# Row statistics finished by GpSimd, and the end of the last sequence's feed-forward part rearranged, in a recurrent fusion and ternary FFN kernel

## The chip, the cores and the metric

The kernel runs on one core of a Trainium2 chip. The metric is the device time of one execution in microseconds; less is better. Of the kernel before there are three timed runs, and one execution under the hardware profiler, from which all durations and instants below come. Instants are microseconds from the start of the profiled span. Engines are named as in the profile: PE (TensorE, matmuls; PEld are its weight loads), DVE (VectorE), ACT (ScalarE), POOL (GpSimd), SP (the engine that issues most DMAs).

## The reference

There are 8 sequences of 512 tokens with 512 features, in f32. In short (shapes left out):

```python
def recurrent(x):                     # both directions, 4 layers, the same weights
    h = x
    for i in range(4):
        z = sigmoid(h @ Wz[i].T + b[i]);  t = tanh(h @ Wh[i].T + b[i])   # Wz = Wh
        a = clip(1 - z, 1e-8, 1 - 1e-8)
        n = linear_scan(a, z * t)     # n[s] = a[s] * n[s-1] + z[s] * t[s]
        h = layernorm(n + (h if i > 0 else 0)) * gamma + beta
    return h
x = x + concat(recurrent(ln(x)), flip(recurrent(flip(ln(x))))) @ fusion_W.T + fusion_b
h = gelu(ln(x) @ ternary(W_fc).T)     # 512 -> 2048
x = x + (layernorm(h) * ln_w + ln_b) @ ternary(W_proj).T
```

`ternary(W)` makes -1, 0 and 1 out of the weights, by half the mean of their absolute values as the threshold. Each layer norm takes the mean and variance of a row (one token, all its features), adds 1e-5 to the variance and raises it to -0.5.

## The kernel before

**First part, to 1222 us: the recurrence and the fusion.** Features lie on the partitions, in four chunks of 128 (`c` or `o`), and the 512 tokens along the free axis, so that the scan of a chunk is one VectorE instruction. Sequences go in pairs; a pair has four streams (two sequences, two directions), and the layers go round the streams. One chunk of a layer is a *step*, in the code a `slot` (L439), about 4.3 us long: TensorE computes `u` (L461), ScalarE makes `a`, `t` and `z` of it (L478 to L480), VectorE clamps `a` (L484), multiplies `z` and `t` (L485), scans (L489) and adds the residual (L548).

The layer norm needs tokens on the partitions. For each of the four token tiles of a stream, TensorE transposes four blocks of `z` into a PSUM tile `pt` (L316, two buffers); VectorE takes `bn_stats` (L171) and `bn_aggr` (L173, `mv` holds mean and variance); then the eps is added (L177, `ve`, VectorE), GpSimd raises to -0.5 (L178, `rs`), VectorE negates the mean (L182, `nmu`), ScalarE multiplies the two (L188, `nmr`) and writes the normalised tile `tok` (L189), which frees `pt`. When four tiles are there, TensorE transposes them back (L325, `pf`), and ScalarE applies gamma and beta on the way to the state (L331). These pieces wait in two queues, `turns` and `backs`, with a due time in steps; `shares` (L258) gives each step one piece of a queue, or two where they are late or the step allows it. The order of all instructions is fixed by this code (a manual schedule); each engine runs its own in order. In a step the queued pieces come after the step's gate matmuls; VectorE does their statistics first and then the step's clamp, product and scan.

Three kinds of statistics go another way: those of x (`rx`, L391) and of the last layer (`rsv`, L354) end with the power and need no shift, and those of y come ahead of the feed-forward part and in it (`y_stats`, L923). The fusion reads `rsv` in L592. Weights are quantised in gaps.

**Second part, from 1222 us: the feed-forward part.** For each sequence `b` and each of 16 chunks `k` of the 2048 features, `fc` (L831) makes `ph` by eight matmuls (L836), then on ScalarE the gelu `g`, its square and the scaled `ghi`, and on VectorE two running sums `acc` (L851) and the rest `glo`. `proj` (L858) multiplies `ghi` and `glo` with the output weights, eight matmuls (L863) into the four token tiles `po`. The loop (L936) runs `fc` two chunks ahead of `proj` (`LAG`); in the last sequence two steps do two `fc` each, so that `token_stats` (L868), which transposes the sums and takes the statistics of the 2048 features, can come two steps before the end. The last two chunks' `proj` goes tile by tile: `center` (L893) has put the mean's part into the rows before, and `finish_last` (L915) adds each tile's scaled `po` and stores it by SP.

Of the kernel before, what the change touches and what calls it, by code (L numbers as in the profile page):

```python
# [9 lines left out]
F32 = mybir.dt.float32  # L10
F32R = mybir.dt.float32r
AF = mybir.ActivationFunctionType
ALU = mybir.AluOpType
# [3 lines left out]
P = 128  # L17
LN_EPS = 1e-5
# [6 lines left out]
def kernel(  # L25
# [26 lines left out]
    nc = tc.nc  # L52
    B, S, H = x.shape
    L = gru_wT.shape[0]
    F = fc_wT.shape[1]
    NC_ = H // P
    NT = S // P
# [6 lines left out]
    const = ctx.enter_context(tc.tile_pool(name="const", bufs=1))  # L64
    small = ctx.enter_context(tc.tile_pool(name="small", bufs=8))
# [11 lines left out]
    fusp = rec.enter_context(tc.tile_pool(name="fus", bufs=1))  # L77
# [29 lines left out]
    gb = const.tile([P, L, NC_], F32, name="gb")  # L107
    gam = const.tile([P, NC_], F32, name="gam")
    bet = const.tile([P, NC_], F32, name="bet")
    fb = const.tile([P, H], F32, name="fb")  # L110
    lnw = const.tile([P, NF], F32, name="lnw")
    lnb = const.tile([P, NF], F32, name="lnb")

# [2 lines left out]
    nc.vector.memset(warm, 0.0)  # L116
    ones = const.tile([P, P], F32, name="ones")
    nc.vector.memset(ones, 1.0)
    both = const.tile([P, NC_, 2, 64], F32, name="both")
    picks = []  # L120
    for i in range(2):
        s = const.tile([P, P], F32, name=f"fpick{i}")
        nc.vector.memset(s, 0.0)
        nc.vector.memset(s[64 * i : 64 * i + 1, :], 1.0 / H if i else 1.0)
        picks.append(s)
# [42 lines left out]
    def stats(src, name, rs=None, shift=True):  # L168

        st = small.tile([P, 6], F32, tag="st", name=f"st_{name}")  # L170
        nc.vector.bn_stats(st, src)  # L171
        mv = small.tile([P, 2], F32, tag="mv", name=f"mv_{name}")
        nc.vector.bn_aggr(mv, st)  # L173
        if rs is None:
            rs = small.tile([P, 1], F32, tag="rs", name=f"rs_{name}")
        ve = small.tile([P, 1], F32, tag="ve", name=f"ve_{name}")
        nc.vector.tensor_scalar(ve, mv[:, 1:2], LN_EPS, None, ALU.add)  # L177
        nc.gpsimd.tensor_tensor(rs, ve, mhalf, ALU.pow)  # L178
        if not shift:
            return rs, None  # L180
        nmu = small.tile([P, 1], F32, tag="nmu", name=f"nmu_{name}")
        nc.vector.tensor_scalar(nmu, mv[:, 0:1], -1.0, None, ALU.mult)  # L182
        return rs, nmu

    def normalise(dst, src, rs_nmu, name):
        rs, nmu = rs_nmu
        nmr = small.tile([P, 1], F32, tag="nmr", name=f"nmr_{name}")
        nc.scalar.activation(nmr, nmu, AF.Copy, scale=rs)  # L188
        nc.scalar.activation(dst, src, AF.Identity, bias=nmr, scale=rs)  # L189

    def ternary(dst, w, hi_lo):
# [11 lines left out]
    def load_y(b):  # L203

        for t in range(NT):
            xs["y", b, t] = xsp.tile([P, H], F32, tag="xs", name=f"xy_{b}_{t}")
            nc.sync.dma_start(out=xs["y", b, t], in_=x1[b][t])
# [3 lines left out]
    def y_chunk(b, toks, c, px):  # L211

        for t in range(NT):
            nc.tensor.transpose(px[:, ts(t, P)], toks[t][:, ts(c, P)], ident)  # L214

        def split():
            hi = zp.tile([P, S], F32R, tag="z", name=f"yhi_{b}_{c}")
            lo = zp.tile([P, S], F32R, tag="z", name=f"ylo_{b}_{c}")
            nc.scalar.copy(hi, px)
            nc.vector.tensor_tensor(lo, px, hi.bitcast(F32), ALU.subtract)  # L220
            ys.setdefault(b, []).append((hi, lo))
        return split
# [6 lines left out]
    with rec:  # L229
# [130 lines left out]
        rx, scale = {}, {}  # L360
# [430 lines left out]


    gpool = ctx.enter_context(tc.tile_pool(name="g", bufs=3, reuse_waits="tile"))
    partp = ctx.enter_context(tc.tile_pool(name="parts", bufs=5, reuse_waits="tile"))
    accp = ctx.enter_context(tc.tile_pool(name="acc", bufs=1, reuse_waits="tile"))
    ps_x = ctx.enter_context(tc.tile_pool(name="ps_x", bufs=2, space=PSUM, reuse_waits="tile"))
    ps_o = ctx.enter_context(tc.tile_pool(name="ps_o", bufs=1, space=PSUM, reuse_waits="tile"))
# [4 lines left out]
    for i in range(2):  # L802
        s = const.tile([P, P], F32, name=f"pick{i}")
# [25 lines left out]
    acc, po, first, stat = {}, {}, {}, {}  # L829

    def fc(b, k):  # L831
        ph = ps_f.tile([P, S], F32, tag="pf", name=f"ph_{b}_{k}")
        for c in range(NC_):
            w = fcq[k // NP_][:, c, ts(k % NP_, P)]
            for i in range(2):
                nc.tensor.matmul(  # L836
                    ph, lhsT=w, rhs=ys[b][c][i], start=(c == 0 and i == 0), stop=(c == NC_ - 1 and i == 1),
                )
        g = gpool.tile([P, S], F32, tag="g", name=f"g_{b}_{k}")
        nc.scalar.activation(g, ph, AF.Gelu)  # L840
        sq = gpool.tile([P, S], F32, tag="sq", name=f"sq_{b}_{k}")
        nc.scalar.activation(sq, g, AF.Square)
        ghi = partp.tile([P, S], F32R, tag="ghi", name=f"ghi_{b}_{k}")
        nc.scalar.activation(ghi, g, AF.Copy, scale=lnw[:, k : k + 1])
        if k == 0:
            first[b] = (g, sq)
        else:
            if k == 1:
                acc[b] = [accp.tile([P, S], F32, tag=f"acc{i}", name=f"acc{i}_{b}") for i in range(2)]
            for i, v in enumerate((g, sq)):  # L850
                nc.vector.tensor_tensor(acc[b][i], first[b][i] if k == 1 else acc[b][i], v, ALU.add)  # L851
        glo = partp.tile([P, S], F32R, tag="glo", name=f"glo_{b}_{k}")
        nc.vector.scalar_tensor_tensor(
            glo, g, lnw[:, k : k + 1], ghi.bitcast(F32), ALU.mult, ALU.subtract
        )
        return ghi, glo
# [11 lines left out]
    def token_stats(b):  # L868

        su = small.tile([P, 2, NT], F32, tag="su", name=f"su_{b}")  # L870
        for i, v in enumerate(acc.pop(b)):
            pst = ps_x.tile([P, 512], F32, tag="px", name=f"pst_{b}_{i}")
            for t in range(NT):
                nc.tensor.transpose(pst[:, ts(t, P)], v[:, ts(t, P)], ident)
            nc.vector.tensor_reduce(su[:, i, :], pst.rearrange("p (t f) -> p t f", t=NT), AX.X, ALU.add)
        nc.vector.tensor_scalar(su, su, 1.0 / F, None, ALU.mult)
        var = small.tile([P, NT], F32, tag="var", name=f"var_{b}")
        nc.vector.tensor_tensor(var, su[:, 0, :], su[:, 0, :], ALU.mult)
        nc.vector.tensor_tensor(var, su[:, 1, :], var, ALU.subtract)
        nc.vector.tensor_scalar(var, var, 0.0, LN_EPS, ALU.max, ALU.add)  # L880
        rs = small.tile([P, NT], F32, tag="rsg", name=f"rsg_{b}")
        nc.gpsimd.tensor_tensor(rs, var, mhalf.broadcast_to([P, NT]), ALU.pow)

        def last():
            nmr = small.tile([P, NT], F32, tag="nmrg", name=f"nmrg_{b}")
            nc.vector.scalar_tensor_tensor(nmr, su[:, 0, :], -1.0, rs, ALU.mult, ALU.mult)
            stat[b] = (rs, nmr)
            if b == B - 1:
                for t in range(NT):
                    center(b, t, xs["y", b, t])  # L890
        return last
# [8 lines left out]
    def store(b, t):  # L900
        nc.sync.dma_start(out=out[b, ts(t, P), :], in_=xs["y", b, t])
# [12 lines left out]

    def finish_last(b, t):  # L915
        row = xs["y", b, t]
        nc.vector.scalar_tensor_tensor(row, po[b][t], stat[b][0][:, t : t + 1], row, ALU.mult, ALU.add)
        store(b, t)

    rests = []  # L920
    found, ytok = {}, {}
# [12 lines left out]
    ends = B * NF  # L934
    todo = [(b, k) for b in range(B) for k in range(NF)]
    for j in range(ends):  # L936
        b, k = divmod(j, NF)
        late = []
        for _ in range(2 if ends - 4 <= j < ends - 2 else 1):
            if todo:  # L940
                waiting.append((*todo[0], *fc(*todo[0])))
                todo.pop(0)
        if j == ends - 2:
            late.append(token_stats(b))
        if k == 0 and b > 0:
            late.append(token_stats(b - 1))
        if b == 0 and 5 <= k < 5 + NC_ + 3:
            row_piece(k - 5)
        if b + 1 < B and k >= NF - NC_:
            px = ps_x.tile([P, S], F32, tag="px", name=f"py_{b + 1}_{k}")  # L950
            late.append(y_chunk(b + 1, ytok[b + 1], k - (NF - NC_), px))
        if j >= LAG:
            done = waiting.pop(0)
            proj(*done)
        for f in late:
            f()
        if rests:
            rests.pop(0)()
        if j >= LAG and done[1] == NF - 1:
            finish(done[0])  # L960
        at = 12 if b == 0 else 8
        if at <= k < at + NT:
            xt = xs["y", b, k - at]
            nc.vector.tensor_tensor(xt, xt, rows[1], ALU.add)
        if b + 1 < B:
            if k == 2:
                load_y(b + 1)
            if k in (6, 7):
                y_stats(b + 1, (2 * k - 12, 2 * k - 11))
            if k in (8, 9):  # L970
                y_tokens(b + 1, (2 * k - 16, 2 * k - 15))
# [47 lines left out]
```

## Time and profile before

| | |
|---|---|
| median of three runs | 1719.33 us (1719.25 to 1719.43) |
| the profiled execution's own time | 1719.44 us |
| its span, first to last instruction | 1717.4 us |
| TensorE clock granted | 1.00 throughout |
| busy: PE / DVE / ACT / POOL | 99% / 84% / 62% / 12% |
| GpSimd's power of a 128x1 tile (L178) | 317 times, about 0.64 us |
| `ve` (L177), `nmu` (L182) on VectorE | 0.15 us, 0.14 us each |
| `nmr` (L188) on ScalarE | 224 times, 0.29 us |

[...]the profile models their ends, so a busy TensorE may still lose time between two matmuls; it shows as a start later than the usual spacing. A line of the timeline gives the start, the duration, the engine, the line of the code, the operation, the tile written and those read, and in brackets the idle time before it and what ended it. A line of the waits gives who waited for whom, the total in us, how often, and the longest.

### The profile page before, as it was taken

The page shows a single profiled execution, that of the slowest core. Times are in us where ns is not written, and L with a number is a line of the kernel's source. Part 1 is how long each engine was busy: PE and PEld are TensorE (multiplying, and loading weights), DVE is VectorE, ACT ScalarE, POOL GpSimd, SP SyncE. Part 2 cuts the span into 40 slices and gives each one's busy share as a digit, 9 for nine tenths or more (in the row PEclk, how much of TensorE's full clock was granted, in tenths as well). Part 3 has the DMA queues.
Part 4 walks back from the last instruction along what each step waited for, and adds up shares of the span by engine and source line. Part 5 has one row for each costly group of instructions (what it writes and reads, how often), then busy time and mean ns, then how long its engine had stood idle before and what let it go on. Part 6 is the DMA issues. An engine that isn't in the chain of part 4 may idle for free.

```text
span 1717.4 us, 19766 instructions
## 1 busy us (share of the span) xinstructions
PE 1705.8 (99%) x6442; PEld 1042.8 (61%) x6442; DVE 1449.8 (84%) x2859; ACT 1072.3 (62%) x1851; POOL 214.5 (12%) x334
## 2 busy tenths in 40 slices
PE   9999999999999999999999999999999999999998
PEld 4455554555555455555545555554688888888887
DVE  7989989889998998999899899996568768768876
ACT  5898883468886246888624688861266566566654
POOL 2111111111111111111111111110000000000000
PEclk9999999999999999999999999999999999999999
DMA  7002221160000115000012200202201101100100
GB/s 270 19 25 81 99 86 43 56 202 1 1 13 19 56 59 199 1 1 19 13 55 68 105 15 35 74 1 98 74 1 49 50 1 50 50 19 32 50 19 31
DMA packets 46455, 91.75 MB, mean 53 GB/s; under 512 B 5264, under 2 KB 5264, under 8 KB 45328
## 3 DMA queue, kind: packets, MB, share of 16 engines
q1 hardware_dynamic: 45632, 89.18, 15.3%
q10 hardware_dynamic: 720, 1.31, 0.2%
q8 instruction: 51, 0.84, 0.2%
q14 instruction: 52, 0.43, 0.1%
HBM read 65.30 MB, written 25.17 MB: 53 GB/s over the span
## 4 chain that ended last, share of the span: by engine, by line
PE 85%; DVE 9%; issue 4%; ACT 1%; DMA 1%; POOL 0%; DVEq 0%; POOLq 0%; ACTq 0%; SPq 0%
PE u L461 33%; PE pu L582 12%; PE ph L836 12%; PE po L863 12%; PE pt L316 6%; PE u L504 5%; PE pf L325 4%; DVE z L489 2%; DVE st L171 1%; DVE z L485 1%; PE py L214 1%; DVE zf L489 1%; DVE z L548 1%; DVE a L484 1%; DMA xT<-in_xt_dram 0%
## 5 line engine op out<-in xcount | busy, mean ns | idle before, releaser
L461 PE MATMUL u<-h,gw 128*128 128x512 f32 x768 | 345.5, 592 | 0.0
L461 PE MATMUL u<-xT,gw 128*128 128x512 f32 x768 | 345.4, 593 | 0.0
L489 DVE TENSOR_TENSOR_SCAN z<-a,z 128x512 f32<-128x512 f32 x224 | 274.1, 1224 | 7.6
L840 ACT ACTIVATE g<-ph 128x512 f32<-128x512 f32 x128 | 76.4, 597 | 240.6 <-PE ph L836 240.6
L461 PEld LDWEIGHTS u<-h,gw 128*128 128x128 f32 x768 | 138.7, 190 | 139.2 <-issue 138.9
L461 PEld LDWEIGHTS u<-xT,gw 128*128 128x128 f32 x768 | 138.7, 190 | 139.2 <-issue 138.2
L478 ACT ACTIVATE a<-u,ngb 128x512 f32<-128x512 f32 x192 | 131.6, 685 | 142.2 <-PE u L461 141.6
L171 DVE BATCH_NORM_STATS2 st<-pt 128x6 f32<-128x512 f32 x256 | 177.1, 692 | 40.5 <-PE pt L316 40.1
L178 POOL TENSOR_TENSOR rs<-ve,mhalf 128x1 f32<-128x1 f32 x192 | 123.2, 642 | 702.8 <-DVE nmu L182 669.9
L863 PE MATMUL po<-pwq,ghi 128*128 128x512 f32 x512 | 203.5, 398 | 0.0
L836 PE MATMUL ph<-yhi,fcq 128*128 128x512 f32 x512 | 199.7, 390 | 0.0
L863 PE MATMUL po<-pwq,glo 128*128 128x512 f32 x512 | 199.6, 390 | 0.0
L836 PE MATMUL ph<-ylo,fcq 128*128 128x512 f32 x512 | 199.4, 389 | 0.0
L485 DVE TENSOR_TENSOR z<-z,t 128x512 f32<-128x512 f32 x224 | 153.4, 685 | 9.1 <-ACT z L480 9.1
L189 ACT ACTIVATE tok<-pt,nmr,rs 128x512 f32<-128x512 f32 x192 | 149.2, 777 | 6.4
L851 DVE TENSOR_TENSOR acc<-acc,g 128x512 f32<-128x512 f32 x112 | 77.3, 690 | 87.9 <-ACT g L840 87.0
L480 ACT ACTIVATE z<-u,gb 128x512 f32<-128x512 f32 x192 | 132.2, 689 | 0.0
L479 ACT ACTIVATE t<-u,gb 128x512 f32<-128x512 f32 x192 | 130.7, 681 | 0.0
L316 PEld LDWEIGHTS pt<-ident,z 128*128 128x128 f32 x640 | 78.6, 141 | 79.7 <-issue 47.7
L504 PE MATMUL u<-xT,gw 128*128 128x512 f32 x256 | 114.8, 593 | 0.8 <-DVE gw L711 0.8
L582 PE MATMUL pu<-fw,xT 128*128 128x512 f32 x256 | 115.2, 593 | 0.0
L582 PE MATMUL pu<-fw,h 128*128 128x512 f32 x256 | 115.1, 592 | 0.0
(147 smaller groups left out, 2558.5 us busy)
## 6 DMA issues: line engine op xcount, KB each, us to landing
xn<-in_x_dram SPq DMA_DIRECT2D x32, 256.0 KB, 4.4
xf<-in_x_dram SPq DMA_DIRECT2D x32, 256.0 KB, 5.5
x<-xf SPq DMA_DIRECT2D x32, 256.0 KB, 2.0
xy<-x SPq DMA_DIRECT2D x32, 256.0 KB, 4.4
out_dram<-xy SPq DMA_DIRECT2D x32, 256.0 KB, 2.0
xT<-in_xt_dram SPq DMA_DIRECT2D x7, 1024.0 KB, 7.5
fca<-in_fc_wT_dram SPq DMA_DIRECT2D x16, 256.0 KB, 3.0
pwa<-in_proj_wT_dram SPq DMA_DIRECT2D x16, 256.0 KB, 2.6
```

The costliest lines, as they stand in the source:

```text
L171: nc.vector.bn_stats(st, src)
L189: nc.scalar.activation(dst, src, AF.Identity, bias=nmr, scale=rs)
L316: nc.tensor.transpose(pt[:, ts(c, P)], zs[c][:, ts(t, P)], ident)
L461: nc.tensor.matmul(u, lhsT=gw[l][:, c, ts(o, P)], rhs=h[:, c, :], start=(c == 0), stop=(c == NC_ - 1),)
L478: nc.scalar.activation(a, u, AF.Sigmoid, bias=ngb[:, l, o : o + 1], scale=-1.0)
L480: nc.scalar.activation(z, u, AF.Sigmoid, bias=gb[:, l, o : o + 1])
L485: nc.vector.tensor_tensor(z, z, t, ALU.mult)
L489: nc.vector.tensor_tensor_scan(dst[:, d], a[:, d], z[:, d], 0.0, ALU.mult, ALU.add)
L504: nc.tensor.matmul(u, lhsT=gw[0][:, c, ts(o, P)], rhs=xT[b][:, c, :], start=(c == 0), stop=(c == NC_ - 1),)
L582: nc.tensor.matmul(pu, lhsT=hs[d][:, c, ts(t, P)], rhs=fw[:, d * NC_ + c, :], start=(c == 0), stop=(c == NC_ - 1),)
L836: nc.tensor.matmul(ph, lhsT=w, rhs=ys[b][c][i], start=(c == 0 and i == 0), stop=(c == NC_ - 1 and i == 1),)
L863: nc.tensor.matmul(po[b][t], lhsT=part[:, ts(t, P)], rhs=pwq[k // NP_][:, k % NP_, :], start=(k == 0 and i == 0), stop=(k == NF - 1 and i ...
```

## The change

Four things change.

- The eps (`ve`) is added by GpSimd for all statistics, in front of its power. The product of mean, `rs` and -1 (`nmr`) is made by GpSimd behind the power, in one instruction; VectorE's `nmu` and ScalarE's `nmr` go. `normalise` keeps only the activation.
- In the last sequence three steps do two `fc` each, in place of two, and one step earlier: `fc` leads `proj` by five chunks at the most. `token_stats` comes three steps before the end. `ghi` and `glo` get a sixth buffer.
- The last token tile is finished in two halves of 256 columns; the second half's store is issued by ScalarE's queue.
- `fb`, `both` and the two `fpick` tiles move from the pool that lasts to the end to one that ends with the first part.

```diff
-    fb = const.tile([P, H], F32, name="fb")
+    fb = fusp.tile([P, H], F32, name="fb")
...
-    both = const.tile([P, NC_, 2, 64], F32, name="both")
+    both = fusp.tile([P, NC_, 2, 64], F32, name="both")
...
-        s = const.tile([P, P], F32, name=f"fpick{i}")
+        s = fusp.tile([P, P], F32, name=f"fpick{i}")
...
         ve = small.tile([P, 1], F32, tag="ve", name=f"ve_{name}")
-        nc.vector.tensor_scalar(ve, mv[:, 1:2], LN_EPS, None, ALU.add)
+        nc.gpsimd.tensor_scalar(ve, mv[:, 1:2], LN_EPS, None, ALU.add)
         nc.gpsimd.tensor_tensor(rs, ve, mhalf, ALU.pow)
         if not shift:
             return rs, None
-        nmu = small.tile([P, 1], F32, tag="nmu", name=f"nmu_{name}")
-        nc.vector.tensor_scalar(nmu, mv[:, 0:1], -1.0, None, ALU.mult)
-        return rs, nmu
-
-    def normalise(dst, src, rs_nmu, name):
-        rs, nmu = rs_nmu
         nmr = small.tile([P, 1], F32, tag="nmr", name=f"nmr_{name}")
-        nc.scalar.activation(nmr, nmu, AF.Copy, scale=rs)
+        nc.gpsimd.tensor_scalar(nmr, mv[:, 0:1], rs, -1.0, ALU.mult, ALU.mult)
+        return rs, nmr
+
+    def normalise(dst, src, rs_nmr, name):
+        rs, nmr = rs_nmr
         nc.scalar.activation(dst, src, AF.Identity, bias=nmr, scale=rs)
...
-    partp = ctx.enter_context(tc.tile_pool(name="parts", bufs=5, reuse_waits="tile"))
+    partp = ctx.enter_context(tc.tile_pool(name="parts", bufs=6, reuse_waits="tile"))
...
     def finish_last(b, t):
         row = xs["y", b, t]
-        nc.vector.scalar_tensor_tensor(row, po[b][t], stat[b][0][:, t : t + 1], row, ALU.mult, ALU.add)
-        store(b, t)
+
+        for h in range(2 if t == NT - 1 else 1):
+            cols = slice(h * H // 2, (h + 1) * H // 2) if t == NT - 1 else slice(0, H)
+            nc.vector.scalar_tensor_tensor(
+                row[:, cols], po[b][t][:, cols], stat[b][0][:, t : t + 1], row[:, cols], ALU.mult, ALU.add
+            )
+            (nc.scalar if h else nc.sync).dma_start(out=out[b, ts(t, P), cols], in_=row[:, cols])
...
-        for _ in range(2 if ends - 4 <= j < ends - 2 else 1):
+        for _ in range(2 if ends - 6 <= j < ends - 3 else 1):
             if todo:
                 waiting.append((*todo[0], *fc(*todo[0])))
                 todo.pop(0)
-        if j == ends - 2:
+        if j == ends - 3:
             late.append(token_stats(b))
```

## The prediction

> **What bounds the kernel now.** I read the page's busy times first, then the waits, then the timeline of one ordinary step, and then listed, from the timeline, every place where TensorE's matmuls start later than their normal spacing.
>
> ```profile
> PE 1705.8 (99%) x6442; PEld 1042.8 (61%) x6442; DVE 1449.8 (84%) x2859; ACT 1072.3 (62%) x1851; POOL 214.5 (12%) x334
> ```
>
> The waits (who waited for whom, us in total, times, longest):
>
> ```profile
> POOL rs L178 <- DVE nmu L182: 669.9, 181, 24.2
> ...
> ACT nmr L188 <- POOL rs L178: 64.9, 49, 7.2
> ...
> PEld pt L316 <- ACT tok L189: 26.7, 86, 0.9
> ```
>
> TensorE is busy 1705.8 of 1717.4 us, and its matmuls follow each other at fixed spacings (429 ns for a 128x512 one with `gw`, 109 ns for a transpose, 227 ns in the feed-forward part). Adding up what exceeds these spacings gives only 17 us: 5.6 before 60 us, 2.3 from there to 120 us, the rest scattered. So there is little to win. What can be lost is in the last line: TensorE waits 86 times for a row tile `tok` that ScalarE makes out of the row statistics. VectorE and GpSimd matter only through that.
>
> ```profile
> 439.81 0.60 PE L325 MATMUL pf<-ident,tok 128*128 128x128 f32 x4
> ...
> 440.75 0.18 DVE L173 BATCH_NORM_AGGREGATE mv<-st 128x2 f32<-128x6 f32 x1
> 441.04 0.15 DVE L177 TENSOR_SCALAR ve<-mv 128x1 f32<-128x1 f32 x1
> 441.11 0.14 DVE L182 TENSOR_SCALAR nmu<-mv 128x1 f32<-128x1 f32 x1
> 441.17 0.42 DVE L484 TENSOR_SCALAR a<-a 128x512 f32<-128x512 f32 x1
> ...
> 441.33 0.65 POOL L178 TENSOR_TENSOR rs<-ve,mhalf 128x1 f32<-128x1 f32 x1 [3.65 <-DVE nmu L182]
> 441.50 0.68 DVE L485 TENSOR_TENSOR z<-z,t 128x512 f32<-128x512 f32 x1
> 442.02 0.29 ACT L188 ACTIVATE nmr<-nmu,rs 128x1 f32<-128x1 f32 x1
> 442.22 1.22 DVE L489 TENSOR_TENSOR_SCAN z<-a,z 128x512 f32<-128x512 f32 x1
> 442.35 0.78 ACT L189 ACTIVATE tok<-pt,nmr,rs 128x512 f32<-128x512 f32 x1
> ```
>
> This is one step (4.31 us), and its neighbours are alike. From the end of `mv` (440.93) to the start of `tok` it takes 1.42 us. The `tok` of the step before ended at 438.82 and was the last of its four; its transpose, the fourth of those from 439.81 on, comes at 440.14, 1.32 us later. This margin is the number that decides.
>
> ```profile
> 38.14 1.21 DVE L489 TENSOR_TENSOR_SCAN z<-a,z 128x512 f32<-128x512 f32 x1
> 38.24 1.45 POOL L178 TENSOR_TENSOR rs<-ve,mhalf 128x1 f32<-128x1 f32 x1 [0.59 <-DVE nmu L182]
> ```
>
> Here the same GpSimd power takes 1.45 us, because it begins inside a scan and ends 0.34 us after it. I paired all 317 powers with the VectorE instruction under way at their start. Beside `bn_stats` (input in PSUM) 81 take 0.55 us. Beside the clamp L484 172 end 0.41 us after its end; so do those beside the products and sums of two SBUF tiles (16 of L851 and L485: 0.9 us).
>
> [...] VectorE shows no price for it: the product after the clamp takes 0.684 us with a power waiting and 0.685 without. [...] three powers in a row at 13.5 us start 0.52 and 0.63 us apart.
>
> **The change, part by part.** The order of instructions on TensorE is unchanged but for eight matmuls near the end; VectorE loses 541 small instructions, ScalarE 224, GpSimd gains 541.
>
> (1) *VectorE and ScalarE are relieved.* Start to start, `mv` to the clamp is 0.42 us now; without `ve` and `nmu` some 0.12: 0.3 us less per statistic. ScalarE loses an `nmr` of 0.29 us. That pays only where they hold TensorE up: around 40 us, and at 72 to 88 us, where two statistics fall in each step and VectorE is full.
>
> (2) *The chain runs through GpSimd three times.* No row shows a GpSimd `tensor_scalar` of 128x1. Bounds: 0.29 us (the affine select of 128x128 on GpSimd) and 0.55 (the power). I take 0.45, 0.31 when it had waited for the port, and 0.06 for the wait on its own result (between 0.03 and 0.14, the handovers seen). With the `mv` end as zero, in the step above: the clamp now runs from -0.08 to 0.34. `ve` starts at 0.13, gets the port at 0.34, is done at 0.65. The power asks at 0.85, while the product runs (0.53 to 1.22, held by ScalarE's `z`), and ends at 1.22+0.41=1.62. `nmr` then asks inside the scan (1.25 to 2.47) and ends at 2.78: `tok` starts at 2.8 in place of 1.42, **1.4 us later**. A shorter instruction hardly helps, since the ends of VectorE's instructions set the times. As `tok` then holds up ScalarE's next gates and so the next product, the power of the next step finds the port free: about 0.7 us. I let 1.4 and 0.7 alternate.
>
> With two statistics in a step (371 us) the first chain runs beside the second's `bn_stats`, but the second queues behind it: its `ve` waits for the scan, its power for the residual sum, and `tok` starts about 4.7 us after the first `mv`, in place of 2.6: **2.0 us later**.
>
> Now the margins. For 47 groups of back transposes (L325 and the first of y) I took the time from the end of the last `tok` to where TensorE would have been free. Five have 0.24 us or less (193, 228, 526, 824, 1126 us): 5.1 us more stall. Four have 0.5 to 0.75: 1.9. Three have 0.89: 0.9. Twenty have about 1.32: nothing or 0.1 each, 1.3. Sum 9.1. For the transposes into a PSUM buffer that `tok` frees, margins are 4.9 us in ordinary steps; they are short where two go in one step. That comes three times, at 321-379, 619-677 and 917-975 us, with margins of -0.2, 0, 0.55, -0.34 and 0.46 us: 0.7+1.5+0.5+1.3+0.2=4.2 each, 12.6 in all (the fourth cut from 2.0, since the stall before it gives time). At 72-110 us the VectorE-bound stall of 0.75 us in a step turns into one on GpSimd of 1.2, and four steps with 0.25 to 0.8 us to spare get one: +4. At 30-52 us 1.1 us is won at the 1.43 us stall on the scan, and lost again at the next `tok`; the first scale comes 0.3 later: 0. Sum 25.7. The margins are those of a trace in which nothing else stalls, and each stall lets the other engines catch up: I take three quarters, **+19.3 us**.
>
> The power for the last layer (`rsv`) is read by L592 at least 1.1 us later, once, else over 5.6: free. The statistics of y in the feed-forward part are used two steps of 3.6 us later: free.
>
> (3) *FC chunks lead by five, token statistics one step earlier.*
>
> ```profile
> 1708.91 2.74 DVE L896 SCALAR_TENSOR_TENSOR xy<-row,nmrg,xy 128x512 f32<-128x512 f32 x4
> ...
> 1711.57 2.72 DVE L917 SCALAR_TENSOR_TENSOR xy<-po,rsg,xy 128x512 f32<-128x512 f32 x4
> ...
> 1712.61 0.39 PE L863 MATMUL po<-pwq,glo 128*128 128x512 f32 x1
> ```
>
> The last matmul ends at 1713.0, VectorE at 1714.29: the four centerings hold it up. They come 1.8 us earlier (eight matmuls of 227 ns), so VectorE follows TensorE. The sixth buffer keeps the lead from waiting. (4) *Last tile in halves*: the second ends at about 1713.1+0.8=1713.9, 0.4 earlier; its store goes past SP on ScalarE's queue, which is idle then, and saves another 0.1 (bounds 0 and 0.3; the store of a whole tile lands in 2.0). Together **-0.5 us**. (5) `fb`, `both` and the picks move to a pool that ends with the first part: no instruction, no wait at the seam (0.4 us there now) that I can see: 0.
>
> Sum: +18.8. The profiled execution took 1719.44 us, 2.1 us outside its 1717.35 of span; the median is 1719.33. So 1719.3+18.8 = **1738**.
>
> **Rivals.** *A, faster, 1716:* GpSimd's small instructions slip between VectorE's, `tok` comes at most 0.2 us later, and the relief decides: -1.8 us at 72-88, -1.5 at the start, -0.9 in the three places, -0.5 at the end, +1 at the five tight groups: -3.7. It decides as long as `mv` to `tok` stays under about 1.7 us. Against it: the 172 powers that did wait for the clamp. *B, same, 1720:* the 1.3 us margin hides nearly all; five tight groups at 1 us cancel against the 4.5 of relief and end. *C, worse, 1761:* shifts of 1.7/1.0, pairs 2.6 us late, and no catching up: 16+19+7=42 us. For it: in a pair step GpSimd needs up to 4.8 us of a 4.75 us step. That part of the edit has no effect is excluded by the instruction order.
>
> **Numbers.** Forecast 0.60 (shift of 1.0/0.5 gives 1728, 1.7/1.0 gives 1751), C 0.16, B 0.13, A 0.11. About 0.2% (3.4 us) can be told from no change. The range leaves out A and the far part of C: 1719 to 1758. Faster 0.11, same 0.13, slower 0.76.
>
> **What would show it.** Right: from `mv` to `tok` 2 us and more; GpSimd's second and third instruction ending 0.3 to 0.4 us after a VectorE product or scan; the wait of `pt` and `pf` for `tok` several times 26.7 us, most of it at 320-379, 619-677, 917-975; VectorE's end 0.4 us nearer to the last matmul. Wrong: `mv` to `tok` near 1.6 us, or that wait unchanged. A stall at the seam near 1222 us would make the layout the cause.

## The result and the profile after

| | before | after |
|---|---|---|
| median | 1719.37 us (1719.25 to 1719.43, 4 runs) | 1739.7 us (1736.4 to 1741.07, 4 runs) |
| the profiled execution's own time | 1719.44 us | 1739.72 us |
| its span | 1717.35 us | 1737.93 us |
| ratio after/before | | 1.0116, 95% interval 1.0098 to 1.0133 |

The changed kernel is 20 us slower. The four runs of after lie further apart than those of before: the mean TensorE clock on record is 0.997 or 0.998 in three of them and 1.000 in the one of 1736.4 us. I come back to that at the end.

In after's code the lines behind the statistics have numbers two lower, up to `finish_last`: the transposes `pt` and the back transposes `pf` are now L314 and L323, `tok` is L187, the clamp, product and scan L482, L483 and L487, the residual L546. `nmr` is now L182, on POOL.

The busy times of after, from its page:

```profile
PE 1710.7 (98%) x6442; PEld 1044.0 (60%) x6442; DVE 1395.0 (80%) x2319; ACT 1009.8 (58%) x1627; POOL 475.3 (27%) x875
```

VectorE lost 55 us of work and ScalarE 62, and GpSimd gained 261. But 317 `ve` at 0.22 us and 224 `nmr` at 0.27, which is what they take with no VectorE instruction beside them (see the durations further down), are only some 130. The other half is not work, it is waiting that the profile counts as busy, because it lies inside the instructions: in the mean the 256 `ve` of the streams take 0.31 us and the 192 `nmr` ahead of `tok` 0.55. TensorE's busy time grew by 5 us only; the span grew by 20.6. So TensorE waits more. The waits of after (who waited for whom, us in total, times, longest):

```profile
POOL ve L177 <- DVE mv L173: 716.5, 210, 22.5
...
ACT tok L187 <- POOL nmr L182: 201.4, 176, 7.6
...
PEld pt L314 <- ACT tok L187: 23.5, 24, 2.2
...
PE pt L314 <- ACT tok L187: 12.8, 14, 2.0
...
PEld pf L323 <- ACT tok L187: 10.4, 10, 2.8
...
PE pf L323 <- ACT tok L187: 8.0, 8, 2.6
```

The matmuls' own waits before:

```profile
PE pt L316 <- ACT tok L189: 2.5, 7, 0.6
...
PE pf L325 <- ACT tok L189: 0.4, 1, 0.4
```

`tok` waits 201 us for the new `nmr`. The weight loads' wait of `pt` for `tok`, which the prediction shows as 26.7 us in 86 waits, is smaller than before, 23.5 us in 24. What grew are the waits on TensorE's own lines: `pt` from 2.5 to 12.8 us and `pf` from 0.4 to 8.0. Together they grew by 17.9 us, most of the 20.6. The weight loads' two lines grew by 5 us only (28.8 to 33.9). They don't tell what was lost: before, they held 28.8 us, while the late starts of all matmuls add up to 17.2 us and the matmuls' own two lines to 2.9.

The same ordinary step in the timeline of after (start, duration, engine, line, operation):

```profile
443.91 0.18 DVE L173 BATCH_NORM_AGGREGATE mv<-st 128x2 f32<-128x6 f32 x1
444.01 0.40 DVE L482 TENSOR_SCALAR a<-a 128x512 f32<-128x512 f32 x1
444.18 0.31 POOL L177 TENSOR_SCALAR ve<-mv 128x1 f32<-128x1 f32 x1 [2.83 <-DVE mv L173]
...
444.54 0.69 DVE L483 TENSOR_TENSOR z<-z,t 128x512 f32<-128x512 f32 x1
444.57 1.09 POOL L178 TENSOR_TENSOR rs<-ve,mhalf 128x1 f32<-128x1 f32 x1
...
445.27 1.22 DVE L487 TENSOR_TENSOR_SCAN z<-a,z 128x512 f32<-128x512 f32 x1
...
445.77 0.80 POOL L182 TENSOR_SCALAR nmr<-mv,rs 128x1 f32<-128x1 f32 x1
...
446.60 0.78 ACT L187 ACTIVATE tok<-pt,nmr,rs 128x512 f32<-128x512 f32 x1 [1.42 <-POOL nmr L182]
...
448.21 0.18 DVE L173 BATCH_NORM_AGGREGATE mv<-st 128x2 f32<-128x6 f32 x1
...
448.87 0.57 POOL L178 TENSOR_TENSOR rs<-ve,mhalf 128x1 f32<-128x1 f32 x1
...
449.14 0.69 DVE L483 TENSOR_TENSOR z<-z,t 128x512 f32<-128x512 f32 x1 [0.44 <-ACT z L478]
...
449.54 0.43 POOL L182 TENSOR_SCALAR nmr<-mv,rs 128x1 f32<-128x1 f32 x1
...
449.87 1.22 DVE L487 TENSOR_TENSOR_SCAN z<-a,z 128x512 f32<-128x512 f32 x1
450.00 0.78 ACT L187 ACTIVATE tok<-pt,nmr,rs 128x512 f32<-128x512 f32 x1 [0.22 <-POOL nmr L182]
```

Each GpSimd instruction begins while a VectorE instruction runs, and ends just after that one's end: `ve` at 444.49 after the clamp (444.41), the power at 445.66 after the product (445.23), `nmr` at 446.57 after the scan (446.49). From the end of `mv` (444.09) to `tok` it is 2.51 us, against 1.42 before. In the next step (448.39 to 450.00) it is 1.61. Over all 192 statistics of this kind the mean is 2.18 us, 1.51 before (the medians are 1.95 and 1.42).

In a step with two statistics (after's timeline; the first `mv` ended at 380.96, this is the chain of the second, whose `mv` ended at 381.83):

```profile
382.78 1.22 DVE L487 TENSOR_TENSOR_SCAN z<-a,z 128x512 f32<-128x512 f32 x1
382.96 1.06 POOL L177 TENSOR_SCALAR ve<-mv 128x1 f32<-128x1 f32 x1
...
384.04 0.69 DVE L546 TENSOR_TENSOR z<-z,xT 128x512 f32<-128x512 f32 x1
384.10 1.05 POOL L178 TENSOR_TENSOR rs<-ve,mhalf 128x1 f32<-128x1 f32 x1
...
385.26 0.27 POOL L182 TENSOR_SCALAR nmr<-mv,rs 128x1 f32<-128x1 f32 x1
...
385.56 0.78 ACT L187 ACTIVATE tok<-pt,nmr,rs 128x512 f32<-128x512 f32 x1 [1.87 <-POOL nmr L182]
...
386.39 0.66 PE L314 MATMUL pt<-ident,z 128*128 128x128 f32 x4 [1.99 <-ACT tok L187]
```

`ve` comes after the first chain's `nmr` (to 382.87) and waits out the scan, the power waits out the residual sum, and TensorE stands for 2 us at `pt`, since `tok` frees its buffer.

Adding up, as in the prediction, how much later than their usual spacing TensorE's matmuls start: 17.2 us before, 38.8 after, +21.6. The tail, from the start of the last matmul to the end of the span, shrank from 4.74 to 4.17 us. Together +21.0; the span says +20.6, and I can't place the 0.4 between them. By place (the rows from lists of the larger stalls, hence 21.2 in sum):

| where | before | after | difference |
|---|---|---|---|
| to 60 us | 5.6 | 6.0 | +0.4 |
| 72 to 110 us, stalls | 2.0 | 5.7 | +3.7 |
| back transposes (`pf` and the first of y), from 120 us | 0.8 | 7.7 | +6.9 |
| the three places with two statistics in a step | 2.1 | 9.5 | +7.4 |
| TensorE at half clock, twice | 0 | 3.4 | +3.4 |
| the tail | 4.74 | 4.17 | -0.6 |

And the end of the span, from after's timeline:

```profile
1733.77 0.39 PE L861 MATMUL po<-pwq,glo 128*128 128x512 f32 x1
1734.19 0.88 DVE L918 SCALAR_TENSOR_TENSOR xy<-po,rsg,xy 128x256 f32<-128x256 f32 x2 [0.15 <-PE po L861]
1735.10 0.35 ACTq L921 DMA_DIRECT2D out_dram<-xy  x1
```

VectorE's last instruction, the second half, ends at 1735.07, 0.9 us after the last matmul (1734.16). Before it was 1.3.

### The profile page after: what moved, and what is told of

It reads as the page before. It is cut to its first block, busy times and chain, and to the rows that moved or that the text cites. A ratio compares the mean times of both kernels' runs of the same rounds, so it can differ in the third digit from the quotient of the medians.

```text
span 1737.9 us, 19487 instructions
## 1 busy us (share of the span) xinstructions
PE 1710.7 (98%) x6442; PEld 1044.0 (60%) x6442; DVE 1395.0 (80%) x2319; ACT 1009.8 (58%) x1627; POOL 475.3 (27%) x875
## 3 DMA queue, kind: packets, MB, share of 16 engines
q10 hardware_dynamic: 864, 1.44, 0.2%
## 4 chain that ended last, share of the span: by engine, by line
PE 53%; issue 24%; POOL 16%; DVE 4%; ACT 2%; POOLq 0%; DVEq 0%
PE u L459 14%; PE po L861 13%; PE ph L834 13%; POOL rs L178 7%; PE pu L580 5%; POOL nmr L182 5%; POOL ve L177 3%; PE pt L314 2%; PE u L502 2%; PE pf L323 1%; PE py L212 1%; DVE z L487 1%; DVE zf L487 1%; ACT tok L187 1%; DVE st L171 1%
## 5 line engine op out<-in xcount | busy, mean ns | idle before, releaser
L487 DVE TENSOR_TENSOR_SCAN z<-a,z 128x512 f32<-128x512 f32 x224 | 274.3, 1224 | 7.5
L177 POOL TENSOR_SCALAR ve<-mv 128x1 f32<-128x1 f32 x256 | 78.5, 307 | 735.7 <-DVE mv L173 716.5
L187 ACT ACTIVATE tok<-pt,nmr,rs 128x512 f32<-128x512 f32 x192 | 149.5, 779 | 201.4 <-POOL nmr L182 201.4
L483 DVE TENSOR_TENSOR z<-z,t 128x512 f32<-128x512 f32 x224 | 154.4, 689 | 43.5 <-ACT z L478 37.4
L178 POOL TENSOR_TENSOR rs<-ve,mhalf 128x1 f32<-128x1 f32 x192 | 148.2, 772 | 16.1 <-POOL ve L177 0.2
L314 PEld LDWEIGHTS pt<-ident,z 128*128 128x128 f32 x640 | 78.5, 141 | 87.6 <-issue 65.3
L323 PE MATMUL pf<-ident,tok 128*128 128x128 f32 x768 | 113.5, 273 | 8.2 <-ACT tok L187 8.0
```

Of the source, the lines that this page charges most:

```text
L483: nc.vector.tensor_tensor(z, z, t, ALU.mult)
L487: nc.vector.tensor_tensor_scan(dst[:, d], a[:, d], z[:, d], 0.0, ALU.mult, ALU.add)
```

## The experiments

The port theory was that of the prediction: a GpSimd instruction that begins beside VectorE's clamp, scan, or product or sum of two SBUF tiles ends only after it, as 172 powers did beside the clamp before (0.41 us after its end), and with three instructions in the chain GpSimd waits up to three times. *Port* is only a name for what it waits for: the traces show the waits and their lengths, and not what lies behind them. The serial theory was its rival: the chain is longer because three GpSimd instructions and two handovers take more time than what they replace, wherever VectorE stands. And the end or the layout of the pools could have been the cause, with the statistics innocent.

**Halving the change.** `e1_end_only` is the changed kernel with the statistics of before; `e2_stats_only` is the kernel before with the statistics of the changed one.

```diff
 e1_end_only, against the changed kernel
-        nc.gpsimd.tensor_scalar(ve, mv[:, 1:2], LN_EPS, None, ALU.add)
+        nc.vector.tensor_scalar(ve, mv[:, 1:2], LN_EPS, None, ALU.add)
...
-        nc.gpsimd.tensor_scalar(nmr, mv[:, 0:1], rs, -1.0, ALU.mult, ALU.mult)
+        nc.vector.tensor_scalar(nmu, mv[:, 0:1], -1.0, None, ALU.mult)
...
+        nc.scalar.activation(nmr, nmu, AF.Copy, scale=rs)
```

> The statistics as before; the five-chunk lead, the sixth buffer, the last tile in halves and the moved pool kept. Port theory (GpSimd's small instructions wait for VectorE's two-input ones) and serial theory (each GpSimd instruction costs alike, whatever VectorE does) both expect 1718.8 us, 0.5 under before, with VectorE's last instruction 0.4 us nearer to the last matmul. Layout theory (the end or the moved pool causes the loss) expects over 1735.

Measured: 1719.15 us (1718.78 to 1720.53), ratio to before 0.9999 (0.9991 to 1.0007).

> The statistics as in the changed kernel, everything else as before. Port and serial theory: 0.5 us over the changed kernel, 1740.2, between 1737 and 1742, the spread being that of the changed kernel. Layout theory: within 1 us of before.

Measured: 1740.82 us (1737.04 to 1741.85), ratio 1.012 (1.0106 to 1.0134). The loss is wholly in the statistics. The end's own gain is too small to be told from nothing here, and the pool layout costs nothing that can be seen.

**Which of the two moves.** `e3_eps_only` moves the eps alone to GpSimd; `e4_product_only` moves the product alone (and drops `nmu` and ScalarE's `nmr`). Both start from the kernel before.

```diff
 e3_eps_only
-        nc.vector.tensor_scalar(ve, mv[:, 1:2], LN_EPS, None, ALU.add)
+        nc.gpsimd.tensor_scalar(ve, mv[:, 1:2], LN_EPS, None, ALU.add)
```

```diff
 e4_product_only
-        nc.vector.tensor_scalar(nmu, mv[:, 0:1], -1.0, None, ALU.mult)
+        nc.gpsimd.tensor_scalar(nmr, mv[:, 0:1], rs, -1.0, ALU.mult, ALU.mult)
...
-        nc.scalar.activation(nmr, nmu, AF.Copy, scale=rs)
```

> Only the eps goes to GpSimd; VectorE negates the mean and ScalarE makes the product, as before. Port theory: ve waits for the clamp and pushes the power into VectorE's product in some steps, but nothing has to get through the scan; from the end of mv to tok 1.4 to 1.9 us, in the median 1.7; time 1723, between 1720 and 1727. Serial theory: one of two added instructions, half of the 20 us, 1729 to 1730.

Measured: 1722.03 us (1721.76 to 1722.36), ratio 1.0014 (1.0008 to 1.0021). From `mv` to `tok` the median is 1.93 us, longer than the 1.7 that the port theory had. The time is close to that theory's and far from the serial one's; the power waits out the product, and then ScalarE makes `nmr`, which takes 0.29 us inside the scan. The timeline of e3:

```profile
442.33 0.69 DVE L485 TENSOR_TENSOR z<-z,t 128x512 f32<-128x512 f32 x1
...
442.56 0.89 POOL L178 TENSOR_TENSOR rs<-ve,mhalf 128x1 f32<-128x1 f32 x1
...
443.06 1.22 DVE L489 TENSOR_TENSOR_SCAN z<-a,z 128x512 f32<-128x512 f32 x1
...
443.49 0.29 ACT L188 ACTIVATE nmr<-nmu,rs 128x1 f32<-128x1 f32 x1 [0.52 <-POOL rs L178]
```

> Only the product of the mean goes to GpSimd, behind the power; VectorE adds the eps as before and has no negation. Port theory: the power ends as before, 1.0 us after mv, so the product asks in VectorE's product or scan and mostly ends behind the scan; mv to tok 2 to 2.7 us; time 1732, between 1728 and 1737, clearly worse than with the eps alone. Serial theory: as with the eps alone, 1729 to 1730.

Measured: 1717.88 us (1717.5 to 1719.54), ratio 0.9993 (0.9984 to 1.0001). Both theories had forecast a loss of 10 us and more, and both were wrong; this kernel is at worst as fast as before. The timeline of e4 shows why:

```profile
444.43 0.42 DVE L482 TENSOR_SCALAR a<-a 128x512 f32<-128x512 f32 x1
...
444.66 0.59 POOL L178 TENSOR_TENSOR rs<-ve,mhalf 128x1 f32<-128x1 f32 x1 [3.35 <-DVE ve L177]
444.78 0.69 DVE L483 TENSOR_TENSOR z<-z,t 128x512 f32<-128x512 f32 x1
...
445.35 0.27 POOL L182 TENSOR_SCALAR nmr<-mv,rs 128x1 f32<-128x1 f32 x1
445.51 1.22 DVE L487 TENSOR_TENSOR_SCAN z<-a,z 128x512 f32<-128x512 f32 x1
445.65 0.78 ACT L187 ACTIVATE tok<-pt,nmr,rs 128x512 f32<-128x512 f32 x1 [0.23 <-POOL nmr L182]
```

The power starts inside the clamp, ends 0.40 us after it (445.25 after 444.85), and so before the product ends (445.47). `nmr` then starts during the product, at 445.35, and ends at 445.62, 0.15 us after the product; the scan starts at 445.51. `nmr` takes 0.27 us, which is what it takes when VectorE is idle (0.27). From this I formed a narrower theory, the gap theory: a GpSimd instruction that asks before one VectorE instruction has ended gets through around its end, and the next VectorE instruction does not push it back; one that asks just after the next has begun waits out the whole of that. If so, it is not the number of GpSimd instructions that decides, but the instant at which each asks, and 0.1 us can be worth a scan.

**Taking the waits away.** The serial theory was still to be excluded for the changed kernel itself. In `e5_psum_after` ScalarE writes the gate `z` into the PSUM tile `u` that it reads. The product and the scan then have one input in SBUF and one in PSUM (192 of the 224 of each; those of the first layer stay as they are); beside `bn_stats`, which reads PSUM, 81 powers took 0.55 us in the kernel before. GpSimd's three instructions and their order stay. `e6_psum_end_only` is the control: the same edit on e1, where the statistics are those of before.

```diff
 e5_psum_after and e6_psum_end_only
-                a, t = factors(u, z, l, o, name)
+                a, t = factors(u, u, l, o, name)
...
-                    product(a, z, t)
-                    scans(a, z)
+                    product(a, u, t)
+                    scans(a, u, z)
...
-                    scan(z, a, z, s[1] == 1)
+                    scan(z, a, u, s[1] == 1)
```

> The changed kernel, with one more edit: after the first layer ScalarE writes the gate z into the PSUM tile u instead of an SBUF tile, so that VectorE's product and scan have one SBUF input each[...]. Nothing of the GpSimd chain is changed. Port theory: GpSimd's power and product no longer wait, mv to tok 1.4 to 1.7 us in the ordinary step in place of 2.3, and most of the loss goes: 1716 to 1724, likeliest 1720. Serial theory: 1737 to 1741 as in the changed kernel, since the three instructions are still there. Open: VectorE may be a little slower with PSUM inputs; 0.05 us more each would not show.

Measured: 1719.35 us (1718.99 to 1721.13), ratio 1.0001 (0.9993 to 1.0009).

> The control: statistics as before, the end as in the changed kernel, and the gate z in PSUM. Both theories: within 1 us of the same kernel without the PSUM edit (1718.8); the few powers that wait for a product or scan (1.45 us at 38 us is in the first layer and stays) win at most 0.5 us.

Measured: 1719.26 us (1719.17 to 1719.62), ratio 0.9999 (0.9991 to 1.0008). The edit by itself moves nothing, and in the changed kernel it takes the whole loss of 20 us away. The timeline of e5, where product and scan now read `u`:

```profile
445.12 0.70 DVE L483 TENSOR_TENSOR u<-u,t 128x512 f32<-128x512 f32 x1
445.17 0.57 POOL L178 TENSOR_TENSOR rs<-ve,mhalf 128x1 f32<-128x1 f32 x1
...
445.84 0.27 POOL L182 TENSOR_SCALAR nmr<-mv,rs 128x1 f32<-128x1 f32 x1
445.86 1.22 DVE L487 TENSOR_TENSOR_SCAN z<-a,u 128x512 f32<-128x512 f32 x1
```

The power runs beside the product in 0.57 us, and `nmr` beside the scan in 0.27, where after's took 1.09 and 0.80. VectorE's product takes 0.70 us with its input in PSUM and the scan 1.22, against 0.69 and 1.22 in after. The chain from `mv` to `tok` takes 1.44 us in the median, against 1.42 before. So without these waits the three GpSimd instructions and their handovers take about as long as the four instructions on three engines that they replace; as the cause of the 20 us the serial theory is out, and GpSimd's waiting during VectorE's product and scan is shown to be that cause. What is left is smaller: the mean of the chain in e5 is still 1.66 us, against 1.51, and e10 below, which differs from e5 only in the eps, is 2.7 us faster. No run tells whether these 2.7 us are the waits that `ve` still has in e5 (146 `ve` take 0.31 us beside the clamp in place of 0.22), or the added instruction itself.

**Is it the gap?** If the gap theory holds, e4 loses its good result when the power is made a little longer. `e8_product_two_columns` is e4 with the eps and the power of a shifted statistic made on two equal columns, of which one is used; it lengthens GpSimd's power by 0.15 us: begun inside the clamp, it ends 0.55 us after it (474.91 after 474.36), where in e4 it was 0.40. `e9_before_two_columns` is the control, the same on the kernel before.

```diff
 e8_product_two_columns and e9_before_two_columns, where a shift follows
-        nc.vector.tensor_scalar(ve, mv[:, 1:2], LN_EPS, None, ALU.add)
-        nc.gpsimd.tensor_tensor(rs, ve, mhalf, ALU.pow)
+            nc.vector.tensor_scalar(ve, mv[:, 1:2].broadcast_to([P, 2]), LN_EPS, None, ALU.add)
+            nc.gpsimd.tensor_tensor(rs2, ve, mhalf.broadcast_to([P, 2]), ALU.pow)
+            rs = rs2[:, 0:1]
```

> The kernel with only the product on GpSimd (1717.9 us), but for tok tiles the eps and the power work on the same variance in two columns instead of one, some 0.15 us more on GpSimd. Gap theory ([...] the product now slips in between VectorE's product and its scan with less than 0.1 us to spare): the product misses that gap and waits out the scan; mv to tok goes from 1.34 to about 2.5 us in the ordinary step, time 1729, between 1724 and 1736. Serial theory: 0.15 us more of a chain with over 1 us of margin, 1717.7 to 1718.6. A theory that blames the eps on GpSimd as such expects the same as the serial one, since the eps stays on VectorE.

Measured: 1732.63 us (1731.9 to 1733.68), ratio 1.0078 (1.0063 to 1.0094).

> The control of the dose: the kernel before with the power in two columns, the product on ScalarE[...]. All theories: mv to tok 0.15 us longer (1.57), time within 0.8 us of before, 1719.4 to 1720.3.

Measured: 1720.55 us (1720.31 to 1720.88), ratio 1.0006 (0.9998 to 1.0014), a little above what was expected. The same 0.15 us costs about 1 us in the kernel before, where no GpSimd instruction follows, and 14.7 us in e4. The timeline of e8:

```profile
473.94 0.42 DVE L489 TENSOR_SCALAR a<-a 128x512 f32<-128x512 f32 x1
...
474.18 0.73 POOL L181 TENSOR_TENSOR rs<-ve,mhalf 128x2 f32<-128x2 f32 x1 [3.10 <-DVE ve L180]
474.27 0.69 DVE L490 TENSOR_TENSOR z<-z,t 128x512 f32<-128x512 f32 x1
...
475.00 1.23 DVE L494 TENSOR_TENSOR_SCAN z<-a,z 128x512 f32<-128x512 f32 x1
475.01 1.27 POOL L189 TENSOR_SCALAR nmr<-mv,rs 128x1 f32<-128x1 f32 x1
...
476.32 0.78 ACT L194 ACTIVATE tok<-pt,nmr,rs 128x512 f32<-128x512 f32 x1 [1.75 <-POOL nmr L189]
```

`nmr` starts 0.01 us after the scan and takes 1.27 us instead of 0.27, ending 0.05 us after the scan. In this step and the next `mv` to `tok` is 2.49 and 1.88 us. The gap theory had forecast the loss (1724 to 1736 us), the serial one had not (at most 1718.6).

**What is worth keeping.** `e7_product_and_end` is the changed kernel with the eps back on VectorE, that is e4 and the new end; `e10_product_end_psum` adds to it the PSUM edit of e5, so that the product no longer depends on the gap.

```diff
 e7_product_and_end and e10_product_end_psum, against the changed kernel
-        nc.gpsimd.tensor_scalar(ve, mv[:, 1:2], LN_EPS, None, ALU.add)
+        nc.vector.tensor_scalar(ve, mv[:, 1:2], LN_EPS, None, ALU.add)
```

> The product of the mean on GpSimd, the eps on VectorE as before, and the end, the sixth buffer and the pool as in the changed kernel. If the two gains add (1.6 us and 0.3 to 0.5 us): 1717.4 us, between 1716.9 and 1717.9, the fastest so far. A theory in which the loss comes from having any further GpSimd instruction behind the power is already ruled out by the run with the product alone.

Measured: 1717.29 us (1717.04 to 1718.54), ratio 0.9988 (0.9982 to 0.9995).

> The product on GpSimd, the end as in the changed kernel, and the gate z in PSUM, so that the gap between VectorE's product and scan no longer matters. Gap theory: in the ordinary step nothing waited there before either, so within 0.7 us of the same kernel without the PSUM edit (about 1717.4).

Measured: 1716.62 us (1716.31 to 1717.87), ratio 0.9984 (0.9978 to 0.9991). This is the fastest version of all, 2.8 us under the kernel before. e7's interval overlaps it, so the PSUM edit's own part of 0.7 us is not certain; that the two together beat the kernel before is. In e7 the gain is scattered: TensorE's gaps add up to 16.3 us in place of 17.2, 0.6 of it between 180 and 240 us, the tail is 4.17 in place of 4.74, and of the 1.85 us by which the span is shorter 0.4 has no place in these sums.

## Why the prediction was right, and where it was not

**The bound.** That TensorE had 17 us of idle time and could lose more than it could win held: what grew in the table above is, from 60 us on, waits of TensorE for `tok` or a consequence of them.

**(1) Relief of VectorE and ScalarE.** Argued to be worth little, and no run shows it to be worth more. e5 keeps all of it and gains nothing. e7 and e10 gain 2 to 3 us with the end included, but they keep it on ScalarE alone (busy 1016.5 us in e7, 1072.3 before); on VectorE only 9 of the 55 us are gone (1440.7).

**(2) The chain through GpSimd.** That GpSimd's instructions wait out VectorE's was right (1.09 us for the power beside the product, 0.80 for `nmr` beside the scan), and e5, where they take 0.57 and 0.27, shows that these waits are the loss. Of its numbers:

- *Durations.* I took 0.45 us for GpSimd's small `tensor_scalar`, and 0.31 after waiting. With no VectorE instruction beside it it takes 0.22 (`ve`) and 0.27 (`nmr`), and after waiting `ve` ends 0.08 us after the clamp and `nmr` 0.07 after the scan. The power's 0.41 was right: 98 powers begun beside the product end 0.43 us after it. The wait on its own result is 0.08 to 0.10 where I took 0.06.
- *The shift.* I had 1.4 and 0.7 us in alternate steps; after shows 1.1 and 0.2 (2.50 and 1.61 against 1.42). The alternation was right, with the reason given for it: at 449.14 the product has waited for ScalarE's `z`, and the power, begun ahead of it at 448.87, took 0.57 us. The sizes are off by the two tails of 0.31 that are 0.07 and 0.08, and in the short steps because `nmr` gets the gap ahead of the scan (449.54 to 449.97, the scan starts at 449.87), which I had not thought of. In the step with two statistics I had 4.7 us from the first `mv` to the second `tok`, and 4.6 came.
- *The margins.* At 72 to 110 us +4 predicted, +3.7 found. The back transposes +9.1 predicted (the four terms, as printed, add up to 9.2), +6.9 found: of the five tight groups three paid 1.5, 0.3 and 0.3 us, one nothing, and that at 1126 us 2.8 (0.5 of it in place of a stall just behind it); of the four with margins of 0.5 to 0.75 two paid 1.3 each and one 0.1; those with 0.89 and 1.32 paid nothing. The three places +12.6 predicted, +7.4 found: I had five late transposes in each, and only one of them, with 2.15 us (386, 687 and 988 us), is large; the others cost 0.3 or 0.4 each. With the factor of three quarters for what the stalls give back, these three terms come to 3.0, 6.8 and 9.4. So the last was the term that was mis-sized: it should have been 7.4. The start, predicted at 0, is +0.4. Sum of the chain's part: 18.4 found, 19.3 predicted.
- *What was missing.* TensorE's half clock, +3.4 us, in no step of the prediction. It made up for what the shift lacked; that the total came out so near owes something to luck. In the one run with a mean clock of 1.000, 1736.4 us, the loss is 17.0 us.

**(3), (4) The end.** -0.5 predicted, -0.6 in the tail of the trace. The last VectorE instruction came 0.4 us nearer to the last matmul, as said, and does so in e1 too. The 0.1 us for the store is not shown: from VectorE's last end to the end of the span it is 3.06 us before, 2.86 in after and 3.13 in e1, which has the same end. In time alone e1 can't show so little.

**(5) The layout.** 0, and e1 with its 0.9999 shows nothing else. The stall at the seam is 0.4 us as before.

**The signs.** `mv` to `tok` of 2 us and more: 2.18 in the mean, but 1.61 in the short steps that alternate with the long ones. GpSimd ending 0.3 to 0.4 us after VectorE's instruction: only the power, 0.43; the other two 0.07 to 0.08. The wait of `pt` and `pf` for `tok` "several times 26.7 us": not so in the line that I named, the weight loads' own, whose two lines came from 28.8 to 33.9 us; so in the matmuls' lines, from 2.9 to 20.8 us. I had chosen a line whose waits cost mostly nothing: 26.7 us before, with TensorE's matmuls 2.5 us late on `pt`. Nor does most of it lie in the three places named: they hold 7.4 of the 18.4 us. VectorE's end: right.

**The rivals.** A ("slip between VectorE's instructions") describes e4, with 1717.9 against its 1716, and not the changed kernel. Its point of decision, `mv` to `tok` under about 1.7 us, held if one takes the mean over the 192 statistics: e4 (1.43 us), e5 (1.66), e9 (1.65), e7 (1.42) and e10 (1.40) lie below it, none more than about 1 us slower than before; after (2.18) and e8 (2.09) lie above. e3 with 1.83 costs 2.6 us only, so the boundary is soft. The medians don't separate the runs: e3, e8 and after have 1.93, 1.93 and 1.95. So it seems to be the latest `tok` tiles that cost time. My evidence against A, that 172 powers had waited for the clamp, was true, but said nothing on the product: which gap is met depends on the chain's phase. Without the eps on GpSimd the phase is the good one (`nmr` takes 0.27 us in e4's step and 0.80 in after's). B (1720) was right for the back transposes with a margin of 1.3 us, which paid nothing, but not for the tight ones and the three places. C (1761) did not come: in each of the three places one stall of 2.15 us is large, and the rest is 0.3 or 0.4.

**What VectorE pays.** Nothing in after or e4 shows it held up by GpSimd: in after 46 clamps start with a GpSimd instruction under way and take 0.39 us like the others, and 169 scans so placed take 1.22 us like the others; in e4 the scan starts 0.04 us after the product's end with `nmr` under way.

## What to carry to other kernels

A short instruction moved to GpSimd cost little here by its own duration (0.22 us for `ve`, 0.27 for `nmr`) and much by the instant at which it asked: `nmr` took 0.27 us when it began ahead of the scan (e4) and 1.27 when it began 0.01 us behind the scan's start (e8). Where TensorE waits for such a chain's end, find for each GpSimd instruction which VectorE instruction runs when it asks (one behind the power was free here, one ahead of it alone cost 2.6 us, both together 20). Taking one input of the long VectorE instructions from PSUM cost nothing here (1719.26 us in e6, 1719.15 in e1) and removed these waits (1719.35 us in e5, 1739.7 in after). What TensorE lost showed in the matmuls' own waits (17.9 us more, of 20.6), not in those of their weight loads (5 us more).

## What was not expected of the hardware

**The clock.** The stretches of after around two stalls (columns: window, its length, busy us and instructions of PE, PEld, DVE, ACT and POOL, granted clock, DMA share, GB/s):

```profile
78.00:82.00 4.00, 3.46 (x8) 2.00 (x9) 2.17 (x5) 2.89 (x5) 2.07 (x5) 0.57 0.00 0
...
1147.00:1151.00 4.00, 4.00 (x7) 1.66 (x6) 3.10 (x4) 1.41 (x3) 0.00 (x0) 0.60 0.00 0
```

In after the clock was halved twice, for 3.41 us each time: from 78.4 to 81.8 us, as a stall of TensorE of 2.15 us ended (at 78.5), and from 1146.8 to 1150.2, 1.2 us after the end of one of 2.77 us (at 1145.6). Matmuls with `gw` then came up to 854 ns apart in place of 429 and in the first stretch transposes 213 in place of 109, 1.7 us lost each time. The stalls of 2.15 us at 386, 687 and 988 us had no such consequence (the granted clock was 1.00 from 386 to 389, from 686 to 690 and from 987 to 991 us), nor one of 2.36 us in e8 (1.000 in the mean of its profiled execution); but one of 1.58 us in e10 did (0.999), and e2 has a stretch of 3.41 us and one of 6.83 at half clock (0.997). So in these traces the length of a stall does not tell whether the clock is halved after it. What does, no run shows.

The clock shows in the spread of after's runs: 1736.4 us at a mean clock of 1.000, 1739.7 at 0.998, 1741.1 at 0.997.

**The size of a dose.** 0.15 us more on GpSimd, in 224 statistics, cost 14.7 us in e4 and about 1 us in the kernel before. I had not expected that one product, moved alone, leaves the time as it was (1.6 us less, at the edge of the noise) or costs 13 us, according to where the power ends.
